# Graph network layer on one core: edge groups taken in pairs, with the order of four engines written out

## The chip, the cores and the metric

The kernel runs on one core of a Trainium2 chip. The metric is the device time of one execution in microseconds (us). The engines are named as in the profile: PE (TensorE; PEld are its weight loads), DVE (VectorE), ACT (ScalarE), POOL (GpSimd), SP (SyncE).

## The reference, cut to what matters

One message passing step over 6250 nodes of 128 features and 100000 edges, whose destinations are sorted, then a node update and a layer norm. All values are float32.

```python
msg_in = concatenate([x[src], x[dst]], axis=-1)      # 100000 x 256
h = relu(msg_in @ Wm1 + bm1)                         # 256 x 256
h = relu(h @ Wm2 + bm2)                              # 256 x 256
messages = h @ Wm3 + bm3                             # 256 x 128
agg = segment_sum(messages, dst, 6250) / clip(count, 1)[:, None]
upd = relu(concatenate([x, agg]) @ Wn1 + bn1) @ Wn2 + bn2
out = layernorm(x + (x + upd))
```

## The kernel before, in words

**Tables.** `Wm1` is split in its source and its destination half and applied to the 6250 nodes instead of the edges. The prologue turns `x` with PE (L263), multiplies (L232) and writes two tables to DRAM: `atab` (float32, one row per node, copied out by ACT, L241) and `btab` (each value as three bf16 terms, L249 to L255: ACT casts the first, DVE subtracts, POOL casts the second, for the last four blocks ACT does that too, DVE subtracts again). It also prepares the node part of the update, `x_part` (L316, with L318 on ACT or L320 on DVE), in thirteen blocks that are placed in lists `X_BESIDE`, `X_BEHIND`, `X_FIRST` and `X_END`: beside the tables, behind them, in the first steps of the loop, and at its end.

**Groups.** The edges are cut in 196 groups of 512 (four columns of 128; the last group is shorter). Since destinations are sorted, a column's edges fall in a window of at most 21 nodes (a loop behind the main one handles wider windows by the data; it has no passes here). For a group:

- POOL gathers the rows of `atab` by the edges' sources: four indirect DMAs of 128 rows into `ag` (L412). SP loads four windows of `btab` into `bw` (L418), with base nodes read into registers. ACT issues the loads of the destinations `db` for two groups at once (L361).
- First layer: PE turns `ag` into `ph` in PSUM (L449, 64-row halves side by side) and adds `bw` times the one-hot `oht` (L455); ACT applies bias and relu (L460) and makes `h1`. DVE makes `oht` (L433) and the one-hot `oh` of the edges (L436).
- Second layer: PE multiplies by `w2` (L469), DVE takes the maximum with minus the bias (L471) into `h2`.
- Sums: PE multiplies by `oh` (L478, four 32-column tiles), which gives the sums of a column's windows in `pg`; ACT copies them to `part` (L481).
- Adding up: PE turns `part` into `pt` in PSUM (L489), and DVE adds windows of `pt` to the accumulator `acc` in SBUF at four dynamic places (L494).

`Wm3` is applied to the sums of `h`, not to the edges, at the end.

**Order.** The loop is unrolled. In iteration `i` the data of group `i` are requested; PE works on group `g = i - 2`. PE's order is the source's (`manual_schedule`); that of DVE and ACT is the source's up to the sixth iteration and then left to the scheduler of the framework, as is POOL's. In an iteration PE does: turned sums of group `g - 4`, first layer of `g`, sums of `g - 3`, second layer of `g - 1`. The buffers: `ag` and `bw` four each, `h2` four; [...] two for `ph`, two for `ph2`, one for `pg`, two for `pt`.

**End.** `products` (L671), `hidden` (L685) and `norm` (L698 to L723) go over 15 blocks of nodes: `Wm3`, division by counts, the update and the layer norm; `norm` lets ACT take the square root and write four pieces `o` (L718), which SP stores.

Of the kernel before, what the change touches and what calls it, by code (L numbers as in the profile page):

```python
# [9 lines left out]
F32 = mybir.dt.float32  # L10
BF16 = mybir.dt.bfloat16
# [8 lines left out]
P = 128  # L20
EPS = 1e-5
NONE = 16384
WN = 32
# [4 lines left out]
def kernel(  # L28
# [16 lines left out]
):  # L45

# [104 lines left out]
    with tc.tile_pool(name="prep", bufs=1) as prep, tc.tile_pool(  # L151
# [74 lines left out]
        LATE = BLOCKS - 4  # L226
# [17 lines left out]
        def b_table(t0):  # L244
# [6 lines left out]
            if t0 < 4 * LATE:  # L251
                nc.gpsimd.tensor_copy(bt[:, :m, 1], rest[:, :m])  # L252
            else:
                nc.scalar.copy(bt[:, :m, 1], rest[:, :m])
# [77 lines left out]
        X_BESIDE, X_BEHIND, X_FIRST, X_END = [0, 1, 2], [3, 4, 5, 6, 7, 8], [9, 12], [10, 11]  # L332
        assert sorted(X_BESIDE + X_BEHIND + X_FIRST + X_END) == list(range(BLOCKS))

        turn(0)
        for i in range(BLOCKS + BEHIND):
# [9 lines left out]
            if i >= BEHIND:  # L346
                for t0 in range(4 * (i - BEHIND), min(4 * (i - BEHIND) + 4, NT), 2):
                    b_table(t0)
            if BLOCKS - 1 <= i < BLOCKS - 1 + len(X_BESIDE):
                whole(x_part(X_BESIDE[i - BLOCKS + 1], bank_pb, (nc.scalar, nc.scalar)))  # L350
# [16 lines left out]
        turns = ExitStack()  # L367
# [3 lines left out]


        PIECE = NPAD // 8
        for c in range(HC + 1):
            for k in range(8):
                nc.gpsimd.memset(acc[:, c, k * PIECE:(k + 1) * PIECE], 0.0)

# [17 lines left out]
    with edge, tc.tile_pool(name="wk", bufs=2) as wk, tc.tile_pool(  # L395
        name="p1", bufs=2, space=PSUM
    ) as p1, tc.tile_pool(name="p2", bufs=2, space=PSUM) as p2, tc.tile_pool(
        name="pa", bufs=1, space=PSUM
    ) as pa, tc.tile_pool(name="pt", bufs=2, space=PSUM) as ptp:


        NH2 = 4
# [4 lines left out]
        def fetch(idx, nt, firsts):  # L407


            ag = ld.tile([P, GT, H], F32, name="ag", bufs=4)  # L410
            for j in range(GT):
                nc.gpsimd.indirect_dma_start(  # L412
                    out=ag[:, j, :], out_offset=None, in_=atab[:, :],
                    in_offset=bass.IndirectOffsetOnAxis(ap=idx[:, j:j + 1], axis=0))
            bw = ld.tile([P, 2, H], BF16, name="bw", bufs=4)
            for j, first in enumerate(firsts):
                terms = btab[ds(first, WB + 1)].rearrange("n c h -> (n c) h")
                nc.sync.dma_start(bw[j // 2 * NQ:(j // 2 + 1) * NQ, j % 2, :], terms[:NQ])  # L418
            return ag, bw
# [7 lines left out]
        def hot(db, pb_cols, dl, nt):  # L427
# [3 lines left out]
            oht = wk.tile([P, 2, P], BF16, name="oht")  # L431
            for k in range(2):
                nc.vector.tensor_scalar(oht[:n, k, :], db[:n, k * P:(k + 1) * P], pb_cols[:n, k:k + 1], None,  # L433
                                        op0=ALU.is_equal)
            oh = wk.tile([P, GT, WN], F32, name="oh", bufs=4)
# [3 lines left out]
            return oht, oh  # L439
# [3 lines left out]
        def first_layer(ag, bw, oht, nt):  # L443
# [14 lines left out]
            for c in range(HC):  # L458
                for h in range(nh):
# [4 lines left out]
        def second_layer(h1, h2, nt):  # L464
            for j0 in range(0, nt, 2):
# [5 lines left out]
                nc.vector.tensor_tensor(h2[:, j0:j0 + 2, :H], ph2, nb2.to_broadcast([P, 2, H]), op=ALU.max)  # L471

        def sums(oh, h2, nt):

            n = nt * WN
            pg = pa.tile([P, H + 1], F32, name="pg")
# [7 lines left out]
        def add_up(part, firsts, nt):  # L484
            pts = [ptp.tile([P, HC + 1, NQ], F32, name="pt") for _ in range(nt // 2)]
            for c in range(HC + 1):
                for h, pt in enumerate(pts):
                    rows = part[halves[h], c * P:(c + 1) * P] if c < HC else part[halves[h], H:].to_broadcast([NQ, P])
                    nc.tensor.matmul(pt[:, c, :], rows, ident[halves[h], halves[h]], is_transpose=True,  # L489
                                     start=True, stop=True, skip_group_check=True)  # L490
            for j, first in enumerate(firsts):
                window = acc[:, :, ds(first, WB)]
                k = j % 2 * WN
                nc.vector.tensor_add(window, window, pts[j // 2][:, :, k:k + WB])  # L494
# [34 lines left out]
        ahead, lag = 2, 3  # L529
        st, hots = {}, {}  # L530
        first = list(X_FIRST)
        for i in range(NG + ahead + 1):
            if i == 6:
                turns.close()
            if i == 16:
# [5 lines left out]
            for step, after in enumerate((20, 24, 27)):  # L541
                if i >= after and (i - after) % 8 == 0 and (i - after) // 8 < len(pieces):
                    double((i - after) // 8, step)
            if i < NG:
                nt = GT if i < NGF else LT
                firsts = load_bases(tilei[0:1, i * GT:(i + 1) * GT], nt, ENG.SP)
                if i == NGF:
                    dbs = last_destinations()
                elif i % 2 == 0:
                    dbs = early.pop(0) if early else destinations(i, min(2, NGF - i), dst_row)  # L550
                st[i] = dict(nt=nt, got=fetch(srcT[:, i, :], nt, firsts), db=dbs.pop(0))
            g = i - ahead
            if 0 <= g < NG:
                s = st[g]
                ag, bw = s.pop("got")

                def make_hot(g):
                    s = st[g]
                    hots[g], s["oh"] = hot(s.pop("db"), pbase[:, g, :], dloc[:, g, :s["nt"]], s["nt"])

                if g not in hots:
                    make_hot(g)
                oht = hots.pop(g)
            k = g - lag - 1
            if 0 <= k < NG:
                s = st.pop(k)
                if "firsts" not in s:
                    s["firsts"] = load_bases(tilei[0:1, k * GT:(k + 1) * GT], s["nt"], ENG.DVE)
                add_up(s["part"], s["firsts"], s["nt"])
            if 0 <= g < NG:  # L570
                s = st[g]
                s["h1"] = first_layer(ag, bw, oht, s["nt"])
                if first:

                    make_hot(g + 1)
                    whole(x_part(first.pop(0), bank_p2, (nc.scalar, nc.vector)))
            k = g - lag
            if 0 <= k < NG:
                s = st[k]
                s["part"] = sums(s["oh"], s["h2"], s["nt"])  # L580
            m = g - 1
            if 0 <= m < NG:
                s = st[m]
                s["h2"] = h2s[m % NH2]
                second_layer(s["h1"], s["h2"], s["nt"])

        with tc.manual_schedule(engines={ENG.DVE, ENG.Activation}):
            rest = (p for b in X_END for p in x_part(b, bank_p1, (nc.scalar, nc.scalar)))
            for k in range(NG - lag, NG):
                s = st[k]  # L590
                s["firsts"] = load_bases(tilei[0:1, k * GT:(k + 1) * GT], s["nt"], ENG.DVE)
            next(rest)
            for k in range(NG - lag, NG):
                s = st[k]
                if k + 1 < NG:
                    st[k + 1]["part"] = sums(st[k + 1]["oh"], st[k + 1]["h2"], st[k + 1]["nt"])
                add_up(s["part"], s["firsts"], s["nt"])
                next(rest)
            assert next(rest, None) is None
            st.clear()  # L600
# [164 lines left out]
```

## Time and profile before

| | |
|---|---|
| three timed runs | 1428.69, 1432.59 (median), 1433.9 us |
| profiled execution, its own time | 1208.8 us |
| its span, first to last instruction | 1207.0 us |
| granted TensorE clock in it | 0.996 |
| main loop, 94 to 1120 us: PE busy | 1025.48 of 1026.00 us |
| the same: DVE, ACT, POOL busy | 546.97, 354.18, 731.84 us |
| the same: DMA share, rate | 0.57, 155 GB/s |
| prologue 0 to 94 us; drain and end 1120 to 1207 us | |

A row of groups in the profile reads: line, engine, operation, output and input names, shapes, count, then busy time in us, mean duration of one in ns, and behind the bar the idle time of the engine just before these instructions with what ended it. Matmuls overlap in the array, so a group's busy time is less than count times mean, and a matmul's pace is the distance from start to start. In a timeline a row is a run of equal instructions: start, length, engine, line, and in brackets the idle time before it with its releaser; "issue" is time in which the engine waited for nothing that the profile shows.

### The profile page before, as it was taken

What the parts mean: (1) busy time and instruction counts of PE and PEld (TensorE: products, weight loads), DVE (VectorE), ACT (ScalarE), POOL (GpSimd) and SP (SyncE); (2) the same over time, 40 slices, a digit from 0 to 9 for tenths busy, and PEclk for the clock granted to TensorE, in tenths of its full rate; (3) what the DMA queues carried; (4) which work ended last, traced back from release to release, by engine and by line L of the source; (5) the groups of instructions that cost most, each with busy time, mean ns of one, the idle gap of its engine ahead of it and who ended that gap; (6) DMA issues with size and microseconds to landing.
All of it is one profiled execution on the core that took longest, in us unless ns stands there. A gap on an engine that the chain in (4) does not pass through costs nothing. (4 is left out here: it accounts for less than half of the span.)

```text
span 1207.0 us, 32797 instructions
## 1 busy us (share of the span) xinstructions
PE 1178.5 (98%) x11196; PEld 895.0 (74%) x11197; DVE 670.4 (56%) x2080; ACT 454.5 (38%) x1163; POOL 804.9 (67%) x859
## 2 busy tenths in 40 slices
PE   7989999999999999999999999999999999999896
PEld 6747777777777777777777777777777777777565
DVE  5864555555555555555555555555555555555586
ACT  5663333333333333333333333333333333333256
POOL 8267777777777777777777777777777777673220
PEclk9999999999999999999999999999999999999999
DMA  8886666666555555555555555555555555552343
GB/s 279 293 261 174 189 180 183 189 191 177 154 151 146 152 153 153 150 152 153 149 148 152 154 154 150 149 152 146 152 153 153 152 152 150 146 148 63 97 111 105
DMA packets 173672, 193.66 MB, mean 160 GB/s; under 512 B 30844, under 2 KB 145486, under 8 KB 173488
## 3 DMA queue, kind: packets, MB, share of 16 engines
q0 software_dynamic: 37984, 103.35, 31.1%
q1 hardware_dynamic: 106956, 61.93, 17.7%
q10 hardware_dynamic: 28564, 26.27, 8.1%
q8 instruction: 90, 1.47, 0.5%
q14 instruction: 78, 0.64, 0.2%
HBM read 168.92 MB, written 22.88 MB: 159 GB/s over the span
## 5 line engine op out<-in xcount | busy, mean ns | idle before, releaser
L412 POOL DMA_INDIRECT ag<-atab,srcT x784 | 752.8, 960 | 282.4 <-issue 184.3
L469 PE MATMUL ph<-w,h 128*128 128x256 f32 x3128 | 727.5, 386 | 1.0 <-ACT x_sb L318 1.0
L469 PEld LDWEIGHTS ph<-w,h 128*128 128x128 f32 x3128 | 578.1, 190 | 152.2 <-DVE acc L494 68.2
L460 ACT ACTIVATE h<-ph,b 128x256 f32<-128x256 f32 x782 | 306.3, 474 | 675.9 <-PE ph L455 495.3
L471 DVE TENSOR_TENSOR h<-ph,nb 128x512 f32<-128x512 f32 x391 | 270.2, 692 | 413.6 <-PE ph L469 411.1
L494 DVE TENSOR_TENSOR acc<-acc,pt 128x63 f32 x782 | 171.7, 220 | 33.9 <-PE ph L455 2.6
L449 PE MATMUL ph<-ident,ag 64*128 64x64 f32 x3128 | 130.3, 223 | 0.6 <-DVE b L382 0.6
L478 PE MATMUL pg<-h,oh 128*32 128x257 f32 x1564 | 125.6, 392 | 0.0
L449 PEld LDWEIGHTS ph<-ident,ag 64*128 64x128 f32 x3128 | 113.5, 139 | 2.7 <-ACT x_sb L318 1.4
L433 DVE TENSOR_SCALAR oht<-db,pbase 128x128 bf16<-128x128 int32 x392 | 104.9, 341 | 1.3 <-PE ph L455 1.0
L489 PEld LDWEIGHTS pt<-ident,part 64*128 64x128 f32 x1173 | 50.9, 136 | 65.9 <-issue 65.2
L455 PE MATMUL ph<-oht,bw 64*128 64x128 bf16 x1564 | 76.6, 217 | 2.7 <-DMA bw<-btab 2.3
L481 ACT COPY part<-pg 128x257 f32<-128x257 f32 x196 | 76.5, 390 | 4.0 <-PE pg L478 4.0
L489 PE MATMUL pt<-ident,part 64*128 64x64 f32 x1173 | 77.8, 238 | 0.2 <-DVE acc L494 0.2
L436 DVE TENSOR_TENSOR oh<-iota_n,dloc 128x128 f32<-128x128 f32 x196 | 55.0, 280 | 20.6 <-PE pg L478 19.7
L676 POOL TENSOR_TENSOR agg<-total,rc 128x512 f32<-128x512 f32 (+2 forms) x15 | 16.0, 1070 | 69.1 <-DVE total L673 65.1
L455 PEld LDWEIGHTS <-bw 64*128 64x128 bf16 x1564 | 53.6, 96 | 3.3 <-DMA bw<-btab 2.6
L232 PE MATMUL pbt<-w,xT 128*128 128x256 f32 x196 | 48.7, 394 | 2.5 <-ACT bt L241 1.6
L478 PEld LDWEIGHTS pg<-h,oh 128*32 128x32 f32 x1564 | 30.8, 108 | 21.7 <-issue 0.8
L232 PEld LDWEIGHTS pbt<-w,xT 128*128 128x128 f32 x196 | 36.8, 197 | 10.9 <-ACT bt L241 2.8
L252 POOL CAST bt<-rest 128x512 bf16<-128x512 f32 x18 | 12.2, 686 | 27.1 <-DVE rest L250 18.0
L698 PEld LDWEIGHTS pot<-wu,u 128*128 128x128 f32 (+1 forms) x196 | 24.0, 191 | 5.5 <-issue 4.8
(109 smaller groups left out, 418.2 us busy)
## 6 DMA issues: line engine op xcount, KB each, us to landing
bw<-btab SPq DMA_DIRECT2D x782, 32.0 KB
db<-in_dst_dram ACTq DMA_DIRECT2D x194, 128.0 KB
ag<-atab,srcT POOLq DMA_INDIRECT x784
btab<-bt SPq DMA_DIRECT2D x24, 384.0 KB
atab<-bt SPq DMA_DIRECT2D x24, 256.0 KB
xd<-in_x_dram SPq DMA_DIRECT2D x12, 256.0 KB
x2tab<-xd SPq DMA_DIRECT2D x12, 256.0 KB
x_sb<-in_x_dram SPq DMA_DIRECT2D x5, 512.0 KB
```

The costliest lines, as they stand in the source:

```text
L232: nc.tensor.matmul(pbt[:, a, :], xT[:, (t0 + a) * P:(t0 + a + 1) * P], w1[:, k, :], start=True, stop=True)
L412: nc.gpsimd.indirect_dma_start(out=ag[:, j, :], out_offset=None, in_=atab[:, :], in_offset=bass.IndirectOffsetOnAxis(ap=idx[:, j:j + 1], a ...
L433: nc.vector.tensor_scalar(oht[:n, k, :], db[:n, k * P:(k + 1) * P], pb_cols[:n, k:k + 1], None, op0=ALU.is_equal)
L449: nc.tensor.matmul(phs[h][:, c, u * NQ:(u + 1) * NQ], ag[halves[h], u, c * P:(c + 1) * P], ident[halves[h], halves[h]], is_transpose=True, ...
L455: nc.tensor.matmul(phs[h][:, c, k * P:(k + 1) * P], bw[halves[h], k, c * P:(c + 1) * P], oht[halves[h], k, :], start=False, stop=True, ski ...
L460: nc.scalar.activation(h1[:, c, h * 2 * P:(h + 1) * 2 * P], phs[h][:, c, :], AF.Relu, bias=b1[:, c:c + 1])
L469: nc.tensor.matmul(ph2[:, a, :], h1[:, c, (j0 + a) * P:(j0 + a + 1) * P], w2[:, c, :], start=(c == 0), stop=(c == HC - 1))
L471: nc.vector.tensor_tensor(h2[:, j0:j0 + 2, :H], ph2, nb2.to_broadcast([P, 2, H]), op=ALU.max)
L478: nc.tensor.matmul(pg[j * WN:(j + 1) * WN, :], oh[:, j, :], h2[:, j, :], start=True, stop=True, skip_group_check=True)
L481: nc.scalar.copy(part[:n, :], pg[:n, :])
L489: nc.tensor.matmul(pt[:, c, :], rows, ident[halves[h], halves[h]], is_transpose=True, start=True, stop=True, skip_group_check=True)
L494: nc.vector.tensor_add(window, window, pts[j // 2][:, :, k:k + WB])
```

## The change

Groups are taken in pairs `a, b = 2i, 2i + 1`, 98 steps. In a step PE does the turned sums of both groups of pair `i - 2`, the first layers of `a` and `b`, the sums of both groups of pair `i - 1`, and the second layers of `a` and `b`. ACT copies the turned sums from PSUM to `col` in SBUF (two copies a pair), and DVE adds from there. `pg` and `pt` share two banks, `ph` gets four. Pair `i + 2` is requested in step `i`: the gathers for its first group after the sums, those for its second group behind a one-element copy on DVE that reads the first half of `h2` of `a` (`gate`). POOL's order is now the source's from the tables on, that of DVE and ACT up to the end of the loop. In the tables' last blocks POOL casts what ACT did, and the first two gathers stand between those casts; one block of `x_part` moves into the first steps. At the end, `norm` is split in three functions, and for the last three blocks the order is written out and DVE writes some of the pieces `o`.

```diff
-            if t0 < 4 * LATE:
-                nc.gpsimd.tensor_copy(bt[:, :m, 1], rest[:, :m])
-            else:
-                nc.scalar.copy(bt[:, :m, 1], rest[:, :m])
+            nc.gpsimd.tensor_copy(bt[:, :m, 1], rest[:, :m])
...
-        X_BESIDE, X_BEHIND, X_FIRST, X_END = [0, 1, 2], [3, 4, 5, 6, 7, 8], [9, 12], [10, 11]
+        X_BESIDE, X_BEHIND, X_FIRST, X_END = [0, 1], [2, 3, 4, 5, 6, 7], [[8], [9, 12]], [10, 11]
...
+        turns.enter_context(tc.manual_schedule(engines={ENG.Pool}))
+        def gather(ag, idx, js):
+            for j in js:
+                nc.gpsimd.indirect_dma_start(
+                    out=ag[:, j, :], out_offset=None, in_=atab[:, :],
+                    in_offset=bass.IndirectOffsetOnAxis(ap=idx[:, j:j + 1], axis=0))
+        def rows_of_a():
+            return ld.tile([P, GT, H], F32, name="ag", bufs=4)
+        first_rows = rows_of_a()
...
+            if i - BLOCKS in (0, 1):
+                gather(first_rows, srcT[:, 0, :], [i - BLOCKS])
...
-        name="p1", bufs=2, space=PSUM
+        name="p1", bufs=4, space=PSUM
     ) as p1, tc.tile_pool(name="p2", bufs=2, space=PSUM) as p2, tc.tile_pool(
-        name="pa", bufs=1, space=PSUM
-    ) as pa, tc.tile_pool(name="pt", bufs=2, space=PSUM) as ptp:
-        NH2 = 4
+        name="pa", bufs=2, space=PSUM
+    ) as pa:
+        NH2 = 2
...
-            for c in range(HC):
-                for h in range(nh):
+            for h in range(nh):
+                for c in range(HC):
                     nc.scalar.activation(h1[:, c, h * 2 * P:(h + 1) * 2 * P], phs[h][:, c, :], AF.Relu,
                                          bias=b1[:, c:c + 1])
...
-        def second_layer(h1, h2, nt):
+        def second_layer(h1, h2, nt, between=None):
...
                 nc.vector.tensor_tensor(h2[:, j0:j0 + 2, :H], ph2, nb2.to_broadcast([P, 2, H]), op=ALU.max)
+                if between and not j0:
+                    between()
...
-            pg = pa.tile([P, H + 1], F32, name="pg")
+            pg = pa.tile([P, H + 1], F32, name="pg", tag="pa")
...
+        def add_up(parts, firsts, nts, between=None):
+            ng = len(parts)
+            pts = [pa.tile([P, ng, HC + 1, NQ], F32, name="pt", tag="pa") for _ in range(max(nts) // 2)]
...
+            for h, pt in enumerate(pts):
+                n = sum(nt // 2 > h for nt in nts)
+                col = wk.tile([P, 2, HC + 1, NQ], F32, name="col")
+                nc.scalar.copy(col[:, :n], pt[:, :n])
+                cols.append(col)
+            if between:
+                between()
...
-                nc.vector.tensor_add(window, window, pts[j // 2][:, :, k:k + WB])
+                    nc.vector.tensor_add(window, window, cols[j // 2][:, s, :, col:col + WB])
...
+        def fetch(g, rows=None, have=(), gate=None):
+            if g % 2 == 0:
+                firsts_of[g // 2] = bases_of(g // 2, ENG.SP)
...
+            ag = rows or rows_of_a()
+            if gate is not None:
+                nc.vector.tensor_copy(ag[0:1, 0, 0:1], gate)
+            gather(ag, srcT[:, g, :], [j for j in range(GT) if j not in have])
+            firsts = firsts_of[g // 2]
+            gots[g] = ag, bases(firsts[:GT] if g % 2 == 0 else firsts[GT:])
...
+        fetch(0, rows=first_rows, have=(0, 1))
+        fetch(1)
+        hot_terms(0)
+        for g, blocks in zip(pair(0), X_FIRST):
+            one_first_layer(g)
+            hot_terms(g + 1)
+            hot_edges(g)
+            for b in blocks:
+                whole(x_part(b, bank_p2, (nc.vector, nc.scalar)))
+            fetch(g + 2, gate=h1s[g][0:1, 0, 0:1])
+            if g == 1:
+                fetch(4)
+            one_second_layer(g)
+        fetch(5, gate=h2s[1][0:1, 0, 0:1])
+        for i in range(1, NS):
...
+            if i + 1 < NS:
+                hot_terms(a + 2)
+            if i >= 2:
+                ps = pair(i - 2)
+                add_up([parts.pop(g) for g in ps], bases_of(i - 2, ENG.DVE), [nts[g] for g in ps])
+            for g in (a, b):
+                one_first_layer(g)
+            for g in pair(i - 1):
+                one_sums(g)
+            if i + 2 < NS:
+                fetch(a + 4)
+            def between():
+                if i + 2 < NS:
+                    fetch(b + 4, gate=h2s[a % NH2][0:1, 0, 0:1])
+                if i + 1 < NS:
+                    hot_edges(a + 2)
+            one_second_layer(a, between)
+            if i + 1 < NS:
+                hot_terms(b + 2)
+                one_second_layer(b, lambda: hot_edges(b + 2))
+            else:
+                one_second_layer(b)
...
+            ends = [(B - 3, [nc.scalar, nc.scalar, nc.scalar, nc.vector]), (B - 2, [nc.scalar, nc.vector]),
+                    (B - 1, [nc.vector, nc.scalar])]
```

`hot_terms` and `hot_edges` make `oht` and `oh` of one group as before, `bases` issues its four `bw` loads, and `one_first_layer`, `one_second_layer` and `one_sums` call the functions of before for one group.

## The prediction

> **What bounds the kernel now.** I read the page first (busy shares, slices, groups), then the granted clock, then the timeline of each engine in one steady step, since the gain or loss of a change of order is read there and not from shares.
>
> ```profile
> PE 1178.5 (98%) x11196; PEld 895.0 (74%) x11197; DVE 670.4 (56%) x2080; ACT 454.5 (38%) x1163; POOL 804.9 (67%) x859
> core 0: 1207.0 us, clock 0.996
> L412 POOL DMA_INDIRECT ag<-atab,srcT x784 | 752.8, 960 | 282.4 <-issue 184.3 <-PE ph L455 80.0 <-PE pg L478 10.3
> ```
>
> PE is busy in 98% of the span, but matmul ends are modelled, so that alone doesn't say that it works at its pace. The starts in the timeline do (start, length, line):
>
> ```profile
> 603.54 0.39 PE L489 MATMUL pt<-ident,part 64*128 64x64 f32 x6
> 603.77 0.66 PE L449 MATMUL ph<-ident,ag 64*128 64x64 f32 x16
> 604.26 0.39 PE L455 MATMUL ph<-oht,bw 64*128 64x128 bf16 x8
> 604.58 0.64 PE L478 MATMUL pg<-h,oh 128*32 128x257 f32 x8
> 605.15 3.72 PE L469 MATMUL ph<-w,h 128*128 128x256 f32 x16
> 608.80 0.40 PE L489 MATMUL pt<-ident,part 64*128 64x64 f32 x6
> ...
> 18.16 3.62 PE L232 MATMUL pbt<-w,xT 128*128 128x256 f32 x16
> 21.61 0.60 PE L263 MATMUL pt<-ident,x_sb 128*128 128x128 f32 x4
> ```
>
> From start to start a group takes 0.23 + 0.49 + 0.32 + 0.57 + 3.65 = 5.26 us. Sixteen matmuls of L469's very shape, L232 in the prologue, take 21.61 - 18.16 = 3.45 us when the line before and after them also uses the whole 128x128 array. So 0.20 of L469's 3.65 us lies at its two borders with lines that use a half (64 rows) or a quarter (32 columns) of the array. PE's limit here is work plus changes of array shape; no wait for another engine stands in these rows. POOL is the next engine:
>
> ```profile
> 604.71 0.95 POOL L412 DMA_INDIRECT ag<-atab,srcT  x1 [0.53 <-PE ph L455]
> 605.97 0.96 POOL L412 DMA_INDIRECT ag<-atab,srcT  x1 [0.30 <-issue]
> 607.23 0.95 POOL L412 DMA_INDIRECT ag<-atab,srcT  x1 [0.30 <-issue]
> 608.48 0.95 POOL L412 DMA_INDIRECT ag<-atab,srcT  x1 [0.30 <-issue]
> 609.98 0.95 POOL L412 DMA_INDIRECT ag<-atab,srcT  x1 [0.54 <-PE ph L455]
> ```
>
> A gather can follow a gather after 1.26 us (0.96 + 0.30 issue): four need 5.04 of the 5.26 us, and POOL then waits for PE to release a buffer. It has only 4% in hand.
>
> **Profiled time and median.** The profiled execution took 1208.8 us at clock 0.996; the three timed runs took 1428.7 to 1433.9 us. If the difference is a slower PE, PE's 1178.5 us were stretched by 223.8 / 1178.5 = 0.19. [...] I keep the measured 0.19: a saving of PE time is multiplied by 1.19, one of fixed latency is not.
>
> **The change part by part** (us at the profiled clock, per pair of groups; 98 pairs, 96 of them full steps).
>
> *PE order.* Not one matmul goes. A step now runs transposes of two groups, first layers of a and b, sums of two groups, second layers of a and b. Transposes: 0.23 + 3 more couples of 0.06 = 0.41. First layer a: 0.49 + 0.23 (eight matmuls of 217 ns spanning 0.39 give 0.057 a couple, and no border to L490 follows); b: 0.49 + 0.32. Sums: a group's two rounds start 0.24 apart and 0.57 = 0.24 + 0.22 + border 0.11; four rounds are 1.03. Second layers: 3.65 + 3.45 = 7.10. Sum 10.07 against 2 x 5.264 = 10.53: 0.46 saved, of which I take 0.45, for 96 steps 43 us. Bounds: 0.25, if the new border between a's bf16 products and b's transposes costs as much as another one (0.1) and the couples don't close up; 0.50, if all borders of one group vanish. I take the upper part since L449 to L455, the same two kinds, already follow each other at 0.06.
>
> *Copies of the transposed sums on ACT.* 196 copies of 128x384. Not in the trace; between `part` L481 (128x257, 0.390) and `bt` L241 (128x512, 0.593): 0.49. ACT rises by 96 us to 46% busy, but they stand ahead of the relus on its queue. With 0 at the step's first transpose: pt ready 0.65, copies end 1.62, two relus for a's first half end 2.45 (four take 1.57), and PE reaches second layer a at 0.41 + 0.72 + 0.81 + 1.03 = 2.97. Cover 0.5 us; each 0.1 beyond it would cost 10 us. Part copies and the db issues (2 x 0.6) follow by 6.6; nothing waits for ACT before 10.7.
>
> *DVE.* The 784 adds (L494, 220 ns, 0.265 apart) now read SBUF twice; nearest row with two SBUF inputs is L436, 280 ns for 128 elements against their 63, so at most 0.22: nothing on DVE. They run from 1.6 to 3.7, ahead of the first max of second layer a at about 5.0; cover 1.3 us. The gate is a 1x1 copy per pair, between the 0.06 of a small memset and the 0.14 of L382: 0.1, on an engine with 4 of 10 us free. Behind it stand one-hot edges and the next max, which PE needs 1.7 us later.
>
> *POOL.* Eight gathers need 10.08 per pair. Run one is released by a's first layer (its last product starts at 1.07; today POOL starts 0.28 after the last L455; so 1.35) and ends at 6.1, run two is gated at about 5.8, so it isn't held, and ends at 11.1, and the next release is at 11.4. POOL and PE would tie at 10.1. What is late next is therefore POOL. Does it lose time to the adds?
>
> ```profile
> 121.99 1.39 POOL L412 DMA_INDIRECT ag<-atab,srcT  x1 [0.30 <-issue]
> ...
> 121.86 0.69 DVE L518 SCALAR_TENSOR_TENSOR xd<-xd,bu 128x512 f32<-128x512 f32 x1 [2.60 <-DMA xd<-in_x_dram]
> ```
>
> This gather took 1.39 instead of 0.96: DVE's L518, with two SBUF inputs, ended 0.56 after its start. [...] By the row, a gather is held once, until the operation in flight ends: with 0.22 us adds 0.1 each, for the one or two gathers that start among them, 0.15. [...] POOL then needs 10.23 at the profiled clock, which would leave 0.30 of the 0.45, 29 us, and a profile near 1208.8 - 29 - 4 = 1176. At the timed runs' pace PE needs 10.07 x 1.19 = 12.0, so the 10.23 are hidden and the full 0.45 counts.
>
> *SP.* Same 782 bw loads, half as many base loads; a group's four issues take 3 us. db is issued by ACT later in a step (5.3), is needed at 0.8 of the next one and can be 1.4 later still before adds delay a max: nothing, and 10 us per 0.1 if it lands after that.
>
> *Ends.* Seven casts (L254, 0.59) move from ACT to POOL in the stretch 63 to 78, where ACT is dense and the first bw load waits for btab (PE waits 2.3 us there): -3, between 0 and -4. The gated gathers of groups 2 to 5 start later than now, and PE may wait 1 or 2 us once: +2. Memsets of acc already run there: 0. The last blocks' output shared by ACT and DVE: -1.5; the drain of the loop: -1.5. Together -4.
>
> **Sum.** 1432.6 - 43 x 1.19 (51) - 4 + 3 for small waits that my 0.5 us covers miss = 1380 us.
>
> **Rivals.**
>
> *As summed, PE keeps the pace* (0.58): 1380, own range 1362 to 1398 (0.35 to 0.55 per pair, ends -10 to +6).
>
> *Gathers, or a thin cover, take part of it back* (0.20). For: the tie at 10.1, ACT's 0.5 us. Against: POOL still waits for PE once in four gathers today, and its slack grows with a slower PE. POOL at 10.23 to 10.40 keeps 0.13 to 0.30 x 96 = 12 to 29 us: about 1412 (1400 to 1422).
>
> *Slower: the timed runs are paced by gathers, not PE* (0.16). The missing 223.8 us spread on 784 gathers are 0.285 each: 1.55 per gather, 12.4 per pair, above PE's 10.07. Then the 0.45 is worth nothing and the adds' 0.15 to 0.3 per pair come on top: 98 x 0.15 to 0.3 = 15 to 29: about 1450. It decides once eight gathers take longer than PE's pair. For: only 4% between them[...]. Against: nothing in the trace stretches a gather but the few rows above, while one slow clock would explain the times.
>
> *No change* (0.06): [...] the compiled order falls apart on a hidden wait of 0.45 per pair. 1433.
>
> Within 0.5% (7 us, about what a measurement of this kernel can tell from no change) lie the last case and a little of the second. Faster by more: 0.58 + 0.20 less 0.03 = 0.75; same 0.09; slower 0.16. The range 1360 to 1436 holds the first two cases but for an edge and nearly all of no change; it leaves out the slower case (0.16) and about 0.03 of the first.
>
> **What would show it.** In the changed kernel's own line numbers (L344 gather, L459 and L465 first layer, L479 second, L490 sums, L505 transposed sums): PE's step from one run of L505 to the next at 10.0 to 10.3 us with 16 + 16 matmuls of L479 in 7.1; L490 once per pair; gathers held by under 0.3 in a pair; ACT's `col` near 0.49 and PE without a wait at L479. Wrong would be: steps of 10.5 or more, PE waits for ag or for h, gathers over 1.1 us on average, or a saving in the profile that the timed runs don't show.

## The result and the profile after

| | median, us | runs, us |
|---|---|---|
| before | 1430.64 | 1427.12 to 1433.9 |
| changed | 1575.95 | 1572.29 to 1582.85 |

Ratio 1.1022, 95% interval 1.0986 to 1.1059: the change is slower by 10%, where 1380 us had been predicted. The chips that the runs met are of two kinds, with the kernel before at 1208 to 1212 us on one (called prompt chips) and at 1430 to 1456 us on the other (late chips). By its times the table above is from late chips; the profile of before, 1208.8 us, is what a prompt chip gives.

The changed kernel's profiled execution took 1575.04 us. Its span and clock, and from its page the engine shares and three rows of groups (columns as told before):

```profile
core 0: 1572.9 us, clock 0.939
```

```profile
PE 1315.7 (84%) x11196; PEld 953.4 (61%) x11197; DVE 700.8 (45%) x2180; ACT 528.2 (34%) x1348; POOL 813.9 (52%) x866
...
L344 POOL DMA_INDIRECT ag<-atab,srcT x784 | 757.1, 966 | 639.7 <-issue 331.5
L479 PE MATMUL ph<-w,h 128*128 128x256 f32 x3128 | 784.8, 398 | 87.8 <-issue 53.0
L511 ACT COPY col<-pt 128x384 f32<-128x384 f32 x196 | 85.1, 481 | 575.7 <-issue 409.0
```

No engine is full: PE 84%, POOL 52%. Matmuls overlap: L479 is busy for 784.8 us, where 3128 x 398 ns would be 1245. A gather takes 966 ns (960 before) and `col` 481 ns, as predicted, but ACT stands idle before `col` for 409.0 us that no wait of the profile explains. One step of the timeline shows where it goes (in this and the later timelines only the rows that bear on the argument stand):

```profile
713.91 0.96 POOL L344 DMA_INDIRECT ag<-atab,srcT  x1 [0.30 <-issue]
714.24 0.58 PE L505 MATMUL pt<-ident,part 64*128 64x64 f32 x12
714.66 0.66 PE L459 MATMUL ph<-ident,ag 64*128 64x64 f32 x16
715.16 0.33 PE L465 MATMUL ph<-oht,bw 64*128 64x128 bf16 x6
715.18 0.96 POOL L344 DMA_INDIRECT ag<-atab,srcT  x1 [0.30 <-issue]
715.94 0.21 PE L465 MATMUL ph<-oht,bw 64*128 64x128 bf16 x1 [0.45 <-issue]
716.65 0.21 PE L465 MATMUL ph<-oht,bw 64*128 64x128 bf16 x1 [0.50 <-issue]
717.36 0.72 PE L459 MATMUL ph<-ident,ag 64*128 64x64 f32 x16 [0.49 <-issue]
717.47 0.86 ACT L511 COPY col<-pt 128x384 f32<-128x384 f32 x2 [5.83 <-issue]
717.86 0.96 POOL L344 DMA_INDIRECT ag<-atab,srcT  x1 [1.72 <-PE ph L465]
...
719.24 1.81 PE L479 MATMUL ph<-w,h 128*128 128x256 f32 x6
720.38 0.96 POOL L344 DMA_INDIRECT ag<-atab,srcT  x1 [0.30 <-issue]
721.39 0.38 PE L479 MATMUL ph<-w,h 128*128 128x256 f32 x1 [0.35 <-issue]
721.65 0.96 POOL L344 DMA_INDIRECT ag<-atab,srcT  x1 [0.30 <-issue]
...
723.51 5.12 PE L479 MATMUL ph<-w,h 128*128 128x256 f32 x23 [0.72 <-issue]
723.64 0.47 ACT L470 ACTIVATE h<-ph,b 128x256 f32<-128x256 f32 x1 [3.83 <-PE ph L479]
723.89 0.69 DVE L481 TENSOR_TENSOR h<-ph,nb 128x512 f32<-128x512 f32 x1 [3.74 <-PE ph L479]
...
728.57 0.58 PE L505 MATMUL pt<-ident,part 64*128 64x64 f32 x12
```

The order of work is the predicted one, but the step takes 14.33 us (714.24 to 728.57), not 10.07. Two things go wrong. The engines that wait for PE start late (in short, PE's signals come late): L505 is over at 714.82, and `col`, which needs nothing else, starts at 717.47, 2.65 us later; the first max (L481) waits until 723.89 for the first eight matmuls of L479, which PE begins from 719.24 on and the last of them at 722.12. And PE itself halts with no wait of its own ("issue"), after 34 matmuls of the step and then in bites of 0.71 us (715.94, 716.65, 717.36). Both end soon after a run of gathers ends: 715.18 + 0.96 = 716.14, and 721.65 + 0.96 = 722.61. A slow clock is no part of this step: the granted clock from 714.24 to 728.57 was 1.00.

### The profile page after: what moved, and what is told of

Read it like the earlier page. It is cut to its first block, busy times and chain, and to the rows that moved or that the text cites. A ratio compares the mean times of both kernels' runs of the same rounds, so it can differ in the third digit from the quotient of the medians.

```text
span 1572.9 us, 32695 instructions
## 1 busy us (share of the span) xinstructions
PE 1315.7 (84%) x11196; PEld 953.4 (61%) x11197; DVE 700.8 (45%) x2180; ACT 528.2 (34%) x1348; POOL 813.9 (52%) x866
## 5 line engine op out<-in xcount | busy, mean ns | idle before, releaser
L479 PE MATMUL ph<-w,h 128*128 128x256 f32 x3128 | 784.8, 398 | 87.8 <-issue 53.0
L479 PEld LDWEIGHTS ph<-w,h 128*128 128x128 f32 x3128 | 597.3, 198 | 292.3 <-issue 123.1
L481 DVE TENSOR_TENSOR h<-ph,nb 128x512 f32<-128x512 f32 x391 | 269.1, 688 | 595.1 <-PE ph L479 330.9
L520 DVE TENSOR_TENSOR acc<-acc,col 128x63 f32 x782 | 180.1, 230 | 226.2 <-issue 171.4
L511 ACT COPY col<-pt 128x384 f32<-128x384 f32 x196 | 85.1, 481 | 575.7 <-issue 409.0
L459 PE MATMUL ph<-ident,ag 64*128 64x64 f32 x3128 | 153.2, 230 | 63.3 <-issue 59.5
L465 PE MATMUL ph<-oht,bw 64*128 64x128 bf16 x1564 | 108.7, 226 | 71.1 <-issue 68.1
L490 PE MATMUL pg<-h,oh 128*32 128x257 f32 x1564 | 146.3, 472 | 12.2 <-issue 11.6
L490 PEld LDWEIGHTS pg<-h,oh 128*32 128x32 f32 x1564 | 48.6, 123 | 60.0 <-issue 35.9
L505 PEld LDWEIGHTS pt<-ident,part 64*128 64x128 f32 x1173 | 43.6, 138 | 33.3 <-issue 32.5
L505 PE MATMUL pt<-ident,part 64*128 64x64 f32 x1173 | 57.0, 230 | 0.0
L251 POOL CAST bt<-rest 128x512 bf16<-128x512 f32 (+1 forms) x25 | 16.9, 683 | 32.5 <-DVE rest L250 21.1
```

The lines of the kernel that those rows point to most:

```text
L459: nc.tensor.matmul(phs[h][:, c, u * NQ:(u + 1) * NQ], ag[halves[h], u, c * P:(c + 1) * P], ident[halves[h], halves[h]], is_transpose=True, ...
L465: nc.tensor.matmul(phs[h][:, c, k * P:(k + 1) * P], bw[halves[h], k, c * P:(c + 1) * P], oht[halves[h], k, :], start=False, stop=True, ski ...
L479: nc.tensor.matmul(ph2[:, a, :], h1[:, c, (j0 + a) * P:(j0 + a + 1) * P], w2[:, c, :], start=(c == 0), stop=(c == HC - 1))
L490: nc.tensor.matmul(pg[j * WN:(j + 1) * WN, :], oh[:, j, :], h2[:, j, :], start=True, stop=True, skip_group_check=True)
L505: nc.tensor.matmul(pts[h][:, s, c, :], rows, ident[halves[h], halves[h]], is_transpose=True, start=True, stop=True, skip_group_check=True)
L511: nc.scalar.copy(col[:, :n], pt[:, :n])
```

## The experiments

Two lengths are read from PE's starts in each trace (medians over the steps): the short part, from the first transpose of `part` to the first matmul of the second layer, and the long part, from there to the next step.

| kernel, chips | short, long, step (us) | time (us) |
|---|---|---|
| before, prompt (per group) | 1.62, 3.65, 5.27 | 1209 |
| before, late (per group) | 2.65, 3.65, 6.30 | 1430 |
| change, prompt | 2.96, 7.11, 10.06 | 1170 |
| change, late | 4.99, 9.11, 14.12 | 1576 |
| late, rows by SP (e11), by plain POOL transfers (e13) | 2.96, 7.11, 10.06 both | 1158, 1160 |
| late, half of the gathers, the change's places (e15) | 2.96, 7.74, 10.70 | 1229 |
| late, half, among the second layers (e16) | 3.41, 7.11, 10.52 | 1212 |
| late, half, begun behind the first layers (e17) | 2.96, 11.03, 13.99 | 1491 |
| late, no gate (e12) | 2.96, 17.02, 19.99 | 2052 |
| late, four runs of two (e14) | 7.45, 7.85, 15.40 | 1685 |
| late, one run of eight (e18) | 8.50, 7.64, 16.45 | 1748 |

**The kernel before, unchanged (e1).**

> The kernel before, unchanged, to learn which time belongs to its trace: the trace shown has 1208.8 us, its timed runs 1430. Theory A (in the timed runs the step is held by waits that the trace shown of before doesn't have, of the kind that the changed kernel's trace shows: PE starts 0.7 us apart with no wait of their own): span about 1430, pair of groups 12.5 us, DVE and ACT durations as before. Theory B (a slower clock in the timed runs): span about 1430 with matmuls of 128x256 more than 216 ns apart and DVE operations longer by the same share. Theory C (the chip differs): span 1207 again, and the changed kernel's loss is then measured against that.

Measured: 1429.92 us, ratio 0.9995 (0.9986 to 1.0004), span 1428.0 us, clock 0.989. Matmuls of the second layer still start 216 ns apart, as in the profile of before. So the 220 us between the profile and the timed runs are no slower clock. Two of its groups in the timeline:

```profile
700.48 0.40 PE L489 MATMUL pt<-ident,part 64*128 64x64 f32 x6
700.71 0.66 PE L449 MATMUL ph<-ident,ag 64*128 64x64 f32 x16
...
701.21 0.55 PE L455 MATMUL ph<-oht,bw 64*128 64x128 bf16 x2
702.25 0.35 PE L455 MATMUL ph<-oht,bw 64*128 64x128 bf16 x6 [0.49 <-issue]
...
706.76 0.40 PE L489 MATMUL pt<-ident,part 64*128 64x64 f32 x6
```

PE halts here too, after 24 matmuls of the group, and a group takes 6.28 us (700.48 to 706.76) instead of 5.27. Nearly the whole loss lies in the short part: 2.65 - 1.62 = 1.03 us, times 195 = 201 of the 221 us.

**No gate (e2, and e12 on another late chip).**

```diff
-            if gate is not None:
-                nc.vector.tensor_copy(ag[0:1, 0, 0:1], gate)
```

> The changed kernel without the one-element copies that gate the second run of four gathers. Theory A (the gate delays gathers or puts DVE between PE and POOL): faster by up to 3 us a pair, 300 us in all, about 1290. Theory B (PE's signals are late for another reason, the gate only follows them): within 3% of 1575.

> The changed kernel without its gate copies, which took 2064 where before takes 1430. Where before takes 1211: if the gate matters only where signals come late, 1165 to 1180, as with the gate (1170); if the gathers' place in a step costs by itself, 1200 to 1500. Where before takes 1430: about 2064 again.

Measured: 2064.33 us, ratio 1.4435 (1.4406 to 1.4464); again 2051.81, ratio 1.41 (1.397 to 1.423). e2 missed both of its expectations: on the late chips the gate, far from being a cost, saves some 490 us. The kernel without it was not run on a prompt chip. POOL works less than half of the time and waits for PE (e12):

```profile
L344 POOL DMA_INDIRECT ag<-atab,srcT x784 | 752.6, 960 | 1117.9 <-PE ph L465 833.6
```

**Only the copies on ACT, in the order of before (e3).**

```diff
+                col = wk.tile([P, HC + 1, NQ], F32, name="col", bufs=4)
+                nc.scalar.copy(col, pt)
...
-                nc.vector.tensor_add(window, window, pts[j // 2][:, :, k:k + WB])
+                nc.vector.tensor_add(window, window, cols[j // 2][:, :, k:k + WB])
```

> The kernel before with one part of the change alone: ACT copies the transposed sums to SBUF (two copies of 128x192 a group) and DVE adds from there. If those copies and the adds with two SBUF inputs are what costs, the time is over 1500. If the pairing of groups is what costs, it stays within 2% of before (1430).

Measured: 1428.99 us, ratio 0.999 (0.9983 to 0.9997). Copies and adds from SBUF cost nothing, on a late chip at that; the loss lies in the rest of the change.

**Rows without gathers (e4, e9, e11; e5 with before; e6 with half).** Theory A is that the gathers hold PE's signals back. Where plain transfers stand in for gathers, here and in e13 and e15 to e17, they bring as many bytes of fixed rows of the table; the edges' own rows are left out, so only the time of these kernels counts.

```diff
-            for j in js:
-                nc.gpsimd.indirect_dma_start(
-                    out=ag[:, j, :], out_offset=None, in_=atab[:, :],
-                    in_offset=bass.IndirectOffsetOnAxis(ap=idx[:, j:j + 1], axis=0))
+            js = list(js)
+            rows = atab[js[0] * P:(js[-1] + 1) * P, :].rearrange("(j p) h -> p j h", p=P)
+            nc.sync.dma_start(ag[:, js[0]:js[-1] + 1, :], rows)
```

> The changed kernel with the table rows of a group brought by one plain transfer of 512 fixed rows on SP's queue (the same 512 KB) instead of four indirect gathers on GpSimd; the rows are therefore not those of the edges. Theory A (GpSimd's gathers, while being issued, hold back the signals by which PE tells the others that it is done): nothing holds them now, so a step of a pair falls from 14.1 us to PE's own 10.1, and the time by 96 x 4.0 = 384 us to about 1190 (1170 to 1240). Theory B (the pair order's own chain transposes, copy, relu, second layer is too long, whatever brings the rows): it stays above 1500. Theory C (it is the bytes on the transfer rings, not GpSimd): about 1576, as the bytes are the same.

> The kernel before with the same replacement: one plain transfer of 512 fixed rows per group on SP's queue for the four gathers. Theory A: a group falls from 6.3 us to PE's 5.27, 196 x 1.1 = 215 us less, about 1210 (1190 to 1240), and the pair order (the run beside this one) is then 10 to 45 us faster than this, as predicted from the trace. Theories B and C: 1430, unchanged.

> The changed kernel with half of the gathers: columns 0 and 1 of a group by GpSimd's gathers, 2 and 3 by one plain transfer of 256 fixed rows on SP's queue (those rows are not those of the edges). Theory A: GpSimd gathers for about 5 of a pair's 10 us and less of the chain meets them; between the two ends, 1250 to 1400. If the delay needs gathers back to back in long runs it is nearly gone: 1200 to 1250. Theories B and C: over 1500.

These met a prompt chip, before at 1211.59 us: e4 1159.14, ratio 0.9579 (0.9551 to 0.9607); e5 1209.45, ratio 0.9983 (0.9973 to 0.9993); e6 1164.37, ratio 0.9622 (0.9594 to 0.965). With the kernel before itself at 1211, none of the three says what a late chip would do. They do say what gathers cost where signals are prompt: 2 us to the old order (1211.59 - 1209.45).

**Four runs of two (e7), and the change itself again (e8).** e7 splits a pair's gathers, the last three couples each behind a gate:

```diff
-                fetch(a + 4)
+                fetch(a + 4, whole_run=False)
...
-                    fetch(b + 4, gate=h2s[a % NH2][0:1, 0, 0:1])
+                    rest_of(a + 4, h2s[a % NH2][0:1, 0, 0:1])
...
+                fetch(b + 4, gate=h2s[a % NH2][0:1, 2, 0:1], whole_run=False)
...
+                    rest_of(b + 4, h2s[b % NH2][0:1, 0, 0:1])
```

> The changed kernel with its eight gathers of a pair in four runs of two, the last three each held by a gate copy (on the first and second half of a's second layer and on the first half of b's). Nothing is left out. Theory A: fewer gathers lie in PE's short instructions at a step's start (transposes and first layers), whose signals the chain needs soonest, so it is faster than the change, 1430 to 1540. Theory B: unchanged, 1570 to 1600. Rival within A: it is the number of gathers under way at all, not where they lie, and the longer gating only makes them end later: 1580 to 1650.

> The changed kernel, unchanged, run again beside the kernel before. The last runs met a chip on which the kernel before takes 1211.6 us, as in the trace that the prediction was read from, and not 1430. Theory D (two chips differ: on one the signals of PE come late while GpSimd gathers, on the other they don't, and the order of pairs suffers more from that than the order of single groups): where before takes 1211, the change takes 1165 to 1185, ratio 0.96 to 0.98; where before takes 1430, it takes 1576 again, ratio 1.10. Theory B (the pair order's chain is too long on any chip): ratio 1.05 or more on either. If it were four runs instead of two that made the run of four runs fast, the change is at 1.02 or more where before takes 1211.

On prompt chips: e7 1171.94, ratio 0.9685 (0.9653 to 0.9717); e8, the unchanged change, 1170.32 beside 1209.12, ratio 0.9674 (0.9658 to 0.969). So the same kernel is 3.3% faster on one kind of chip and 10% slower on the other. Its timeline there:

```profile
600.90 0.58 PE L505 MATMUL pt<-ident,part 64*128 64x64 f32 x12
601.32 0.66 PE L459 MATMUL ph<-ident,ag 64*128 64x64 f32 x16
601.38 0.96 POOL L344 DMA_INDIRECT ag<-atab,srcT  x1 [0.30 <-issue]
601.56 0.86 ACT L511 COPY col<-pt 128x384 f32<-128x384 f32 x2 [5.73 <-PE pt L505]
601.81 0.39 PE L465 MATMUL ph<-oht,bw 64*128 64x128 bf16 x8
602.04 0.66 PE L459 MATMUL ph<-ident,ag 64*128 64x64 f32 x16
602.54 0.39 PE L465 MATMUL ph<-oht,bw 64*128 64x128 bf16 x8
602.85 1.07 PE L490 MATMUL pg<-h,oh 128*32 128x257 f32 x16
603.86 7.17 PE L479 MATMUL ph<-w,h 128*128 128x256 f32 x32
610.96 0.58 PE L505 MATMUL pt<-ident,part 64*128 64x64 f32 x12
```

610.96 - 600.90 = 10.06 us per pair, no wait and no halt, with POOL gathering throughout. `col` starts 0.08 us after L505 ends (600.90 + 0.58 = 601.48), where the late chip had 2.65. Against e4, gathers cost the new order 1170 - 1159 = 11 us here.

**Both runs gated (e10), and e4 again (e9).**

```diff
-                fetch(a + 4)
...
-                    fetch(b + 4, gate=h2s[a % NH2][0:1, 0, 0:1])
+                    fetch(a + 4, gate=h2s[a % NH2][0:1, 0, 0:1])
...
+                    fetch(b + 4, gate=h2s[b % NH2][0:1, 0, 0:1])
```

> The changed kernel once more with a group's table rows brought by one plain transfer of 512 fixed rows on SP's queue instead of GpSimd's gathers, to be read beside the kernel before on the same chip. Where before takes 1430: if GpSimd's gathers are what holds PE's signals back there (theory A), 1160 to 1200; if that chip delays signals whatever is gathered, or the bytes do it (theory C), 1400 to 1600. Where before takes 1211: 1159 again, which tells nothing new.

> The changed kernel with both runs of four gathers held by a gate copy: the first on the first half of a's second layer, the second on the first half of b's. Nothing is left out. Where before takes 1211: the first run begins 4.5 us later in a step but the eight still fit behind one another in 10.1 us, and buffers come free as before: 1165 to 1185, or up to 1230 if GpSimd's 10.1 of 10.1 us can no longer be made up for. Where before takes 1430: if the delay comes from gathers under way during the transposes and first layers, the first 4 us of a step are now freer of them and it falls below the change's 1576, 1430 to 1540; if it comes from gathers anywhere, 1560 to 1700.

A prompt chip again (before 1207.95): e9 1158.84, ratio 0.9586 (0.9551 to 0.962); e10 1174.09, ratio 0.9712 (0.9674 to 0.975). On such a chip the three places tried lie within 4 us (1170, 1172, 1174). e10 was not run on a late chip.

**No gathers on a late chip (e11).**

> The changed kernel with a group's table rows brought by one plain transfer of 512 fixed rows on SP's queue instead of GpSimd's gathers, for a third time, since the chip on which before takes 1430 has not been met again. Where before takes 1430: theory A (GpSimd's gathers hold PE's signals back) 1160 to 1200, otherwise 1400 to 1600. Where before takes 1211: 1159.

Beside a before of 1456.16 us: 1158.27, ratio 0.796 (0.793 to 0.7989). This decides. Without GpSimd's gathers the changed kernel takes on a late chip (1158 us) what it takes on a prompt one (1159 in e4 and e9). Theory B (the chain of the pair order is too long) falls, and so does theory C (the bytes moved), since the bytes were the same. That SP issues the transfers, and fewer of them, also differs here; e13 puts POOL and the 784 transfers back.

**Plain transfers by POOL (e13), four runs (e14) and half (e15) on a late chip.**

```diff
-                nc.gpsimd.indirect_dma_start(
-                    out=ag[:, j, :], out_offset=None, in_=atab[:, :],
-                    in_offset=bass.IndirectOffsetOnAxis(ap=idx[:, j:j + 1], axis=0))
+                nc.gpsimd.dma_start(ag[:, j, :], atab[j * P:(j + 1) * P, :])
```

> The changed kernel with each gather replaced by a plain transfer of 128 fixed rows, still issued by GpSimd at the same place (784 of them; the rows are not those of the edges). If any transfer that GpSimd issues holds PE's signals back: where before takes 1430 to 1456 this takes 1450 to 1600. If it is the indirect addressing: 1160 to 1200. Where before takes 1211: 1160 to 1175.

> The changed kernel with its eight gathers of a pair in four runs of two, three of them gated, once more (1172 where before takes 1211, as the change). Where before takes 1430 to 1456: if the place of the gathers in a step decides, 1430 to 1530, below the change's 1576; if their number does, 1560 to 1620.

> The changed kernel with two of a group's four gathers replaced by one plain transfer of 256 fixed rows on SP's queue, once more (1164 where before takes 1211). Where before takes 1430 to 1456: if each gather costs its share, half of the loss is left, about 1158 + (1576 - 1158) / 2 = 1367; if only gathers back to back in long runs cost, 1160 to 1230.

Beside a before of 1432.66: e13 1160.17, ratio 0.8099 (0.8076 to 0.8123); e14 1685.47, ratio 1.1766 (1.1716 to 1.1816); e15 1229.02, ratio 0.858 (0.8555 to 0.8605). Rows of e13's groups:

```profile
L344 POOL DMA_DIRECT2D ag<-atab x784 | 416.1, 538 | 563.1 <-PE ph L463 260.5 <-issue 258.9 <-PE ph L477 17.6
L479 DVE TENSOR_TENSOR h<-ph,nb 128x512 f32<-128x512 f32 x391 | 270.8, 692 | 352.5 <-PE ph L477 352.4
```

As many transfers issued by POOL at the same places, and nothing is late. So it is the indirect gather, not POOL's issuing as such; whether its addressing, its longer hold of POOL (0.96 against 0.54 us) or its scattered rows, these runs don't tell. e15's loss is (1229 - 1158) / (1576 - 1158) = 0.17 of the change's for half of the gathers: the loss doesn't go with their number. It was expected so if only long runs of gathers cost, but e14, with all gathers in runs of two, speaks against that. e14 missed both of its expectations: the gates push the last gathers into the next step's short part, which grows to 7.45 us.

**Place against number, with half of the gathers (e16, e17).** Four gathers a pair in both, held by one gate at different places (the other half as in e6):

```diff
e16:
+                    fetch(g, gate=h1s[b][0:1, 1, 2 * P:2 * P + 1])
e17:
+                    fetch(g, gate=h2s[b % NH2][0:1, 2, 0:1])
```

> The changed kernel with half of the gathers (the other half as one plain transfer of fixed rows per group on SP's queue), all four of a pair in one run that a gate copy holds until the relus of b's first layer are done: they run from about 4 to 9 us of a step, beside the 32 long matmuls of the second layers alone. Where before takes 1430 to 1456: if the loss comes from gathers that meet PE's short instructions, it is gone, 1158 to 1180; if it goes with the number of gathers, 1229 as with half of them in the change's own places. Where before takes 1211: 1164.

> The same half of the gathers in one run that a gate copy holds until the last max of b: they run from about 0.3 to 5.3 us of the next step, over all of its short instructions. Where before takes 1430 to 1456: if the loss comes from gathers that meet PE's short instructions, it is larger than in the change's places, 1280 to 1450; if it goes with their number, 1229. Where before takes 1211: 1164 to 1175.

Beside a before of 1451.65: e16 1211.7, ratio 0.8343 (0.829 to 0.8396); e17 1491.43, ratio 1.0269 (1.0201 to 1.0337). As many gathers, 280 us apart: with half of them, place rules. Neither was run on a prompt chip. e16, then e17:

```profile
699.46 0.95 POOL L344 DMA_INDIRECT ag<-atab,srcT  x1 [5.81 <-DVE ag L587]
...
700.82 0.69 DVE L483 TENSOR_TENSOR h<-ph,nb 128x512 f32<-128x512 f32 x1 [0.67 <-issue]
...
703.24 0.95 POOL L344 DMA_INDIRECT ag<-atab,srcT  x1 [0.30 <-issue]
704.17 0.58 PE L507 MATMUL pt<-ident,part 64*128 64x64 f32 x12
...
705.80 0.86 ACT L513 COPY col<-pt 128x384 f32<-128x384 f32 x2 [6.25 <-PE pt L507]
```

```profile
700.61 0.96 POOL L344 DMA_INDIRECT ag<-atab,srcT  x1 [9.26 <-PE ph L467]
...
701.86 3.72 PE L481 MATMUL ph<-w,h 128*128 128x256 f32 x16
...
704.40 0.96 POOL L344 DMA_INDIRECT ag<-atab,srcT  x1 [0.30 <-issue]
706.75 0.69 DVE L483 TENSOR_TENSOR h<-ph,nb 128x512 f32<-128x512 f32 x1 [3.84 <-PE ph L481]
707.59 3.69 PE L481 MATMUL ph<-w,h 128*128 128x256 f32 x16 [2.01 <-DVE h L483]
```

In e16 the gathers lie beside L481 alone and end at 704.19, just as the short part begins at 704.17: the max shown comes after a wait of 0.7 us, `col` starts 1.05 us after L507 ended. That isn't the 1158 to 1180 expected of this place: some 50 us of loss are left against the 1164 that half of the gathers, in the change's places, took on a prompt chip (e6), most of it in the short part (3.41 against 2.96 us). In e17 they begin at 700.61, not 0.3 but 1.7 us into the step (the buffers come free only with b's first layer), among the last of the 60 short matmuls of transposes and first layers; the first max of L481 then starts at 706.75, although its eight matmuls were begun from 701.86 on (216 ns apart), and only 1.39 us after the last gather ended. PE waits 2.01 us for that max. My expectation had the place of the run wrong and its direction right; the 1491 us lie above its 1280 to 1450.

**All eight in one run from that late place (e18).**

```diff
-                fetch(a + 4)
+                fetch(a + 4, gate=h1s[b][0:1, 1, 2 * P:2 * P + 1])
+                fetch(b + 4)
...
-                    fetch(b + 4, gate=h2s[a % NH2][0:1, 0, 0:1])
```

> The changed kernel with all eight gathers of a pair in one run of 10.1 us, held by one gate copy on the relus of b's first layer (about 4 us into a step). Nothing is left out. Where before takes 1430 to 1456: if the place rules with eight as with four, only the last gathers of the run meet the next step's short instructions, where the change's first run begins among them each time: 1350 to 1480, near or below before; if with eight there is no good place left, 1560 to 1750. Where before takes 1211: the run fills the step, 1170 to 1195, as the change (1170) or a little more.

Beside a before of 1450.2: 1747.67, ratio 1.2045 (1.2024 to 1.2065). It was meant to beat both kernels and is the slowest gated one:

```profile
706.05 0.58 PE L505 MATMUL pt<-ident,part 64*128 64x64 f32 x12
706.07 0.95 POOL L344 DMA_INDIRECT ag<-atab,srcT  x1 [0.30 <-issue]
706.46 1.02 PE L459 MATMUL ph<-ident,ag 64*128 64x64 f32 x16
...
708.59 0.96 POOL L344 DMA_INDIRECT ag<-atab,srcT  x1 [0.30 <-issue]
709.32 0.28 PE L465 MATMUL ph<-oht,bw 64*128 64x128 bf16 x3 [1.19 <-issue]
...
711.44 0.30 PE L465 MATMUL ph<-oht,bw 64*128 64x128 bf16 x4 [1.84 <-issue]
711.55 0.69 PE L459 MATMUL ph<-ident,ag 64*128 64x64 f32 x16
711.60 0.86 ACT L511 COPY col<-pt 128x384 f32<-128x384 f32 x2 [11.72 <-remote]
...
712.55 1.94 PE L490 MATMUL pg<-h,oh 128*32 128x257 f32 x16
```

Eight gathers (10.1 us) don't fit between the short parts: the last three meet the next one. PE halts after 28 matmuls, and `col` starts 4.97 us after L505 ended. A second loss follows the halts: the granted clock was 1.00 until they end at 711.44, then 0.62 until 714.42, and the sums (L490) take 1.94 us instead of the 1.07 of e8. Over the whole run the clock was 0.845, and it was 0.85 in e14 and without the gate too, so their losses are not late signals and halts alone. In the steps shown of the change, e1 and e17 it was 1.00. With all gathers no place tried on a late chip beats before.

## Why the prediction was wrong

- **PE order.** Wrong on the late chips (14.1 us, above the 10.5 that the prediction had set as its limit), right where signals are prompt: 10.07 us per pair predicted, 10.06 measured in the median step of e8 (10.11 in the mean).
- **ACT copies, adds, gate.** Right in size: 0.481 us (0.49), adds 0.227 (up to 0.22), gate 0.14 (0.1). e3 shows the copies at nothing, as predicted.
- **POOL and the adds.** Mis-sized on the safe side. The 0.15 us per pair, an estimate from one gather beside L518, isn't in the median step, which stays 10.06, and 6 of 784 gathers take over 1.1 us (7 before). In the trace of before the five gathers that begin under L518 take 1.15 to 1.39 us, longer the more of L518 is left (0.32 to 0.56 us). Beside the adds with two SBUF inputs nothing of the kind shows in the mean: a gather takes 961 ns (e8), 960 without them (before).
- **Ends.** Mis-sized: -4 predicted, +4 to +9 measured. The span falls by 37.3 us (1207.0 to 1169.7, e8); the full steps save 96 x 0.48 = 46 us by their median and 96 x 0.43 = 41 us by their mean. PE waits 2.0 us for gated gathers in the first steps, as estimated. The first transpose of `part` comes at 115.3 instead of 107.8 us, but in the new order one more second layer and one more set of sums stand ahead of it, some 4.2 us of work; with the rows by SP (e9) it comes at 108.1. The rest I have not taken apart.
- **Profiled time and median: the step that failed.** "If the difference is a slower PE, PE's 1178.5 us were stretched by 0.19." e1 has nearly the same clock (0.989 against 0.996) and the same pace of matmuls (216 ns), and loses 1.03 us per group in the short part, to halts of PE. I took a profile at 1208.8 us for a scaled picture of runs at 1432 us. It showed the machine without the very thing that the change makes worse: in the new order late signals and halts take 4.06 us per pair (14.12 - 10.06), where the sum, scaling PE's work by 1.19, had the pair order ahead by 51 us.
- **The rival "slower, paced by gathers"** named the right culprit with the wrong mechanism: it stretched each gather by 0.285 us, but gathers take 966 ns against 960. They don't pace the kernel by their own length; PE's signals come late beside them. Its 1450 was too low for that reason, and that it had the sign right was luck.
- **The sum in its right form**, late chips: where signals are prompt the new order gains 1209 - 1170 = 39 us. A late chip adds 1430 - 1209 = 221 us to the old order and 1576 - 1170 = 406 us to the new one; -39 + 185 = +146 us. For the new order e11 and e13 show that the indirect gathers are the cause; for the old order, where PE halts in the same way (e1), this is argued. Of the 406, two parts of about 2.0 us a pair are read in the table: 4.99 - 2.96 in the short part, 9.11 - 7.11 in the long one, times 97 = 391. The first transpose of `part` also comes 16 us later (131.4 against 115.3). The old order loses almost only in its short part, 2 x 1.03 a pair.

## What to carry to other kernels

Where the profiled execution and the timed runs of one kernel differ by 18%, no sum can be scaled across the gap: profile the kernel unchanged until a trace has the timed pace, and read that one. Replacing a suspect transfer by a plain one of the same bytes (e11, e13) separates its cost from the order's in one run. Where indirect gathers run beside PE, the place of a gather relative to PE's bursts of short matmuls can weigh more than its number (half of the gathers in both, 1212 us in e16 and 1491 in e17); and an order that is faster on one chip (ratio 0.967) should be timed on a second (1.102 here).

## What the runs showed of the hardware

- Chips differ in this (before takes 1208 to 1212 or 1430 to 1456 us): two prompt and four late ones were met in the experiments, and the one of each kind that was met twice kept its kind. Why they differ stays open.
- On a late chip, while indirect gathers are issued, ACT and DVE start late after the matmuls that they wait for: `col` by 2.6 us (change) and 4.7 us (e18), the first max of a step by 2.1 us (change), 2.9 (e17) and 5.8 (e12), all medians. On a prompt chip (e8), and on a late one without indirect gathers (e11, e13), it is under 0.1 us for both. And PE halts after 24 (e1) to 42 (e14) matmuls of a step, in bites of about 0.7 us. Once a run of gathers has ended, PE or the late engine goes on within 0.9 to 2.1 us (after, e17, e18). After PE's long halts in the step shown of e18 the granted clock was 0.62. Gathers that begin behind the short matmuls delay the second layers (the long part is 11.03 us in e17 and 17.02 in e12, against 7.11 in e11 without gathers); gathers that run into them stop PE itself (the short part is 7.45 us in e14 and 8.50 in e18, against 2.96); gathers beside long matmuls alone do little (e16, half of the gathers: 3.41 and 7.11 us). By what mechanism gathers do this was not shown.
- Not tried: the kernel before without gathers on a late chip, and gathers of consecutive rows.
